# A perceiver kernel: float32r parts for the first ternary product, and fewer steps around keys, norms and value biases

## The chip, the cores and the metric

The kernel runs on one core of a Trainium2 chip. The metric is device time in microseconds of one execution of the whole program, as the median of the runs; the profile is of one further execution, taken by the hardware profiler. Engines are named as in the profile: PE (TensorE, matmuls; PEld its weight loads), DVE (VectorE), ACT (ScalarE), POOL (GpSimd), SP (SyncE, which only issues DMAs here).

## What is computed

A latent array x (128 batches, 32 rows, 256 columns) and a context (128 batches, 257 rows, 256 columns) go through two layers of three residual steps each:

```python
x = x + xattn0(context, LN(x))     # softmax attention of 32 rows on 257 context rows
x = x + ssm(LN(x))                 # gated selective scan over the 32 rows, 512 channels, 16 states
x = x + ffn0(LN(x))                # gelu(LN(x) @ Q(W_fc).T), layernorm, @ Q(W_proj).T; Q is ternary
x = x + xattn1(LN(x), context)     # linear attention with a focused feature map, 16 heads
x = x + attn1(LN(x))               # latent attention with a distance decay
x = x + ffn1(LN(x))                # 8-bit activations, ternary weights, gelu
```

Two pieces matter most for the change. The focused feature map of xattn1, on queries and keys alike, is

```python
x = relu(x) + 1e-6
x = x / softplus(scale)
n = norm(x)                 # along the 256 columns
x = x ** 3 / norm(x ** 3) * n
```

and its output is `q @ (k.T @ v) / (q . sum(k) + 1e-6)`, where `v = context @ Wv + bv`. In ffn0 the weight matrix W_fc is replaced by -1, 0 and 1 before the first product, so only the activations carry many significant bits. Inputs and outputs are float32.

## The kernel before

**Units of work.** Four batches of 32 latent rows make a *group* of 128 rows, one per partition; there are 32 groups. Groups are put together in blocks of 2, 4, 4, 4, 4, 4, 4, 4 and 2 (`BLOCKS`). For each block the program lists: for every group `context_group` (line 993: xattn0, and the keys and values of xattn1 reduced to a small tile `kvc`); then one `scan_block` (1155) for the block; then for every group `latent_group` (1471), which is `mlp` (1223, ffn0), `linear` (1259, the query side of xattn1), `attention` (1310) and `quantized_mlp` (1441). Weight preparation stands in front, and `late_setup` (882) after the first block's context.

**The order is planned ahead.** Nothing is issued when it is listed. A `Recorder` (267) notes every operation with the engines that may do it, a time for each from `ns_of` (42), and the regions of tiles that it reads and writes. `order` (403) then lays all operations out with a list scheduler that follows its own clock: each part of the work has a due time in the table `DUE`, an operation whose earliest start lies within `WINDOW` of the first possible one competes by due time, and an operation that may run on several engines goes to the one with the smallest start plus time x (1 + `PRICE`). The result is one fixed sequence per engine, and `trace` (566) issues it; the line of every such instruction is therefore 575, and the groups of the profile are told apart by tile names. `keep_busy` (553, issuing at line 562) puts dummy matmuls into gaps of PE that the planner sees as longer than 600 ns.

**Buffers.** Tiles come from rings: `t1` of 7 buffers of 1 KB a partition, `t2` of 17 of 2 KB, `t4` of 4 of 4 KB, eight PSUM banks, and small ones. How early a piece of work can begin depends also on a free buffer of its ring.

**The steps that the change touches.**
- Keys (`keys`, 1102, and `keys_values`, 1121): the product of context and key weights for one batch fills a bank (`pkey`, 128x512). The bias goes in first, as a matmul of three bf16 rows `bk3` with ones. Then `relu` on ACT into `ku`, POOL adds `e1` (1e-6 over the softplus), and `cubed` (765) follows: two squares on ACT with a sum each, the cube on POOL, two squares again, then one POOL power over the four sums `kn` (exponents 0.5 and -0.5) and one POOL product to `kf`. ACT scales the values by it into `vf`, and PE adds keys times values into `pk`.
- `kvc` is formed from `pk` on DVE; the value bias is applied later, in `linear`: DVE copies the denominators to `den`, POOL multiplies `bv1` by them, and DVE adds the numerators and multiplies by the reciprocal `zf`.
- Norms: `stats` (961) takes mean and variance on DVE, `rstd_of` (955) makes the reciprocal root in two POOL steps, and `norm` (969) applies both on DVE into `xn`. This happens for every group in the scan, in attention and in the quantized MLP.
- First ternary product (`mlp`, 1223): the centred rows are transposed by PE, copied by ACT to `xT`, and split into three bf16 parts `x3` (two casts on ACT or POOL, two subtractions on POOL). PE multiplies each part by the ternary weights, kept in bf16.

The matmuls of that product read, for each half of the 1024 columns,

```python
(x3[:, k3, dc * P : (dc + 1) * P], w_fc[:, dc, cols])
for dc in range(2) for k3 in range(3)
```

- `quantize` (1409): `qm` is 127 over the largest magnitude (a reciprocal and a multiply on DVE); for 256 columns DVE scales and rounds and POOL takes the rounding constant away again.

Of the kernel before, what the change touches and what calls it, by code (L numbers as in the profile page):

```python
# [9 lines left out]
BF16 = mybir.dt.bfloat16  # L10
I32 = mybir.dt.int32
# [255 lines left out]
class Recorder:  # L267
# [62 lines left out]
    def record(self, calls):  # L330
        ways = {}
        for engine, (name, args, kw) in calls.items():
            out = kw.get("out", args[0] if args else None)
            rest = list(args[1:] if "out" not in kw else args)
            rest += [v for k, v in kw.items() if k not in ("out", "accum_out")]
            ins = [a for a in rest if is_ap(a)]
            outs = [a for a in (out, kw.get("accum_out")) if is_ap(a)]
            full = dict(kw)
            if name == "tensor_scalar":
                full |= dict(zip(("scalar1", "scalar2"), args[2:4]))  # L340
            if name == "scalar_tensor_tensor":
                full |= dict(zip(("scalar",), args[2:3]))
            if name == "activation":
                full |= dict(zip(("func",), args[2:3]))
            if engine == "gpsimd" and name == "tensor_tensor":
                full |= dict(zip(("op",), args[3:4]))
            n = size_of(out)
            ns = ns_of(engine, name, full, out, ins, n)
            table = TABLES.get(full.get("func")) if name == "activation" else None
            tensors = [  # L350
                a for a in ins if (size_of(a) > 1 or name == "tensor_tensor") and not in_psum(a)
            ]
            locks = engine == "gpsimd" and len(ins) > 0
            if engine == "vector":
                two = name in ("tensor_tensor", "scalar_tensor_tensor", "tensor_tensor_scan")
                fast = name in ("tensor_scalar", "tensor_copy") and not in_psum(out)
                locks = len(tensors) > 1 if two else fast and len(tensors) > 0 and n > 64
            ways[engine] = [(name, args, kw)], ns, locks
        reads = [b for b in map(box_of, ins) if b]
        writes = [b for b in map(box_of, outs) if b]  # L360
        bufs = [a.buf for a in (*ins, *outs) if isinstance(a, View)]
        self.keep += bufs
        self.bufs_of.update((id(b), b) for b in bufs)
        if self.joined is not None:
            small = ins[0].shape[0] < P or size_of(ins[0]) < P
            self.joined.append((*ways["tensor"][:2], reads, writes, small))
            return
        landing = 0
        if "sync" in ways:
            size = size_of(out) * P * 4 if writes else 0  # L370
            landing = 2000 + size / 180.0
        self.add(ways, reads, writes, table, landing)
# [218 lines left out]
PRICE = {"tensor": 0.0, "vector": 28.013093, "scalar": 4.356996, "gpsimd": 3.720234, "sync": 0.0}  # L591
WINDOW = 13.821085
SOONER = 0.0675
AHEAD = 0.744939
HORIZON = 1.665209
# [3 lines left out]
def perceiver_kernel(ctx: ExitStack, tc: tile.TileContext, t: dict, out: bass.AP):  # L599
# [30 lines left out]
    nc.gpsimd.memset(halves[:, 1, :], 0.5)  # L630
    ones = cst.tile([P, P], F32, name="ones")
# [61 lines left out]
    def t2k(shape, name, dtype=F32):  # L693
        return ring("t2", 17).tile(shape, name, dtype)
# [33 lines left out]
    bv1 = row("bv1", t["bv1"], D)  # L728
# [17 lines left out]
    w_fc = wts.tile([P, 2, HID], BF16, name="w_fc")  # L746
# [18 lines left out]
    def cubed(u, n, tag, inverse=False):  # L765
# [8 lines left out]
        powers = halves[:, 0:2, 0:n] if inverse else halves[:, 1:3, 0:n]  # L774
        R.gpsimd.tensor_tensor(nrm, nrm, powers, ALU.pow)
        f = tiny(f"{tag}f", [P, n])
        R.gpsimd.tensor_tensor(f, nrm[:, 0, :], nrm[:, 1, :], ALU.mult)
# [59 lines left out]
    R.vector.tensor_tensor(bk, bk, col, ALU.mult)  # L837

    parts = t1k([P, 2, 4, 32], "bkp")
    R.gpsimd.memset(parts, 0.0)  # L840
    for k in range(3):
        part = ring("bkb", 1).tile([P, 2], "bkb", BF16)
        R.vector.tensor_copy(part, bk)
        R.vector.tensor_copy(parts[:, :, :, k], part.unsqueeze(2).to_broadcast([P, 2, 4]))
        if k < 2:
            R.vector.tensor_tensor(bk, bk, parts[:, :, 0, k], ALU.subtract)
# [24 lines left out]
    R.vector.tensor_scalar(p_l[:, 0, :], pkl[:, 0:D], 0.0, None, ALU.max)  # L871
    R.vector.tensor_tensor(p_l[:, 0, :], p_l[:, 0, :], e1, ALU.add)
# [88 lines left out]
    def stats(xg):  # L961

        st = tiny("st", [P, 6])
        R.vector.bn_stats(st, xg)
        mv = tiny("mv", [P, 2])
        R.vector.bn_aggr(mv, st)
        return mv, rstd_of(mv[:, 1:2], LN_EPS)

    def norm(xg):
        mv, r = stats(xg)  # L970
        xn = t1k([P, D], "xn")
        R.vector.tensor_scalar(xn, xg, mv[:, 0:1], r, ALU.subtract, ALU.mult)
        return xn, mv, r
# [19 lines left out]
    def context_group(b0, xg, kvc):  # L993
# [91 lines left out]
        with R.together():  # L1085
            for m in range(8):
# [6 lines left out]
                )  # L1093
        for b in range(0, GB, PAIR):
            zs = keys(cTs[b : b + PAIR])
            for i in range(PAIR):
                keys_values(cTs[b + i], zs[i], pk[:, :, b + i, :], b + i == GB - 1)
        v = pk.rearrange("p c b (h k) -> p h c b k", h=2)
        R.vector.tensor_scalar(kvc, v[:, 0], odd[:, 0:1], None, ALU.mult)
        R.vector.scalar_tensor_tensor(kvc, v[:, 1], odd[:, 1:2], kvc, ALU.mult, ALU.add)  # L1100

# [19 lines left out]
    def keys_values(cT, z, pk, last):  # L1121
        u = t2k([P, 2, D], "ku")
        R.relu(u, z)
        R.gpsimd.tensor_tensor(u, u, e1.unsqueeze(1).to_broadcast([P, 2, D]), ALU.add)
        f = cubed(u, 2, "k")
        R.first = (len(R.ops) - 3,)
# [10 lines left out]
        for j in range(2):  # L1137
            R.scalar.activation(
                vf[:, j, :, 0:16], pv[:, j * D : (j + 1) * D].rearrange("p (h k) -> p h k", k=16),
                AF.Copy, scale=f[:, j : j + 1],  # L1140
            )
        R.gpsimd.tensor_copy(vf[:, :, :, 16], f.unsqueeze(2).to_broadcast([P, 2, NH]))
        with R.together():
            for c in range(2):
                for j in range(2):
                    for m in range(4 * c, 4 * c + 4):
# [5 lines left out]
                        )  # L1152


    def scan_block(x, late):
# [3 lines left out]
        xT = ring("xTs", 1).tile([P, 2, TOK], "xTs")[:, :, 0:tok]  # L1159
        for g in range(size):  # L1160
            xn, _, _ = norm(x[g])
            R.gpsimd.tensor_tensor(x[g], x[g], b_out, ALU.add)
            transposed(xn, xT[:, :, g * P : (g + 1) * P], 2)
# [59 lines left out]
    def mlp(xg):  # L1223
# [3 lines left out]
        xT = t1k([P, D], "xT")  # L1227
        transposed(xc, xT.rearrange("p (c n) -> p c n", c=2), 2)

        x3 = t2k([P, 3, D], "x3", BF16)  # L1230
        R.cast(x3[:, 0, :], xT)
        R.gpsimd.tensor_tensor(xT, xT, x3[:, 0, :], ALU.subtract)
        R.cast(x3[:, 1, :], xT)
        R.gpsimd.tensor_tensor(x3[:, 2, :], xT, x3[:, 1, :], ALU.subtract)
# [3 lines left out]
        for k in range(2):  # L1238
            ph = bank("ph")
            cols = slice(k * 512, (k + 1) * 512)  # L1240
            with R.together():
                accumulate(ph, [
                    (x3[:, k3, dc * P : (dc + 1) * P], w_fc[:, dc, cols])
                    for dc in range(2) for k3 in range(3)
                ])
# [13 lines left out]
    def linear(xg, kvc):  # L1259
# [32 lines left out]
        den = tiny("den", [P, NH], 2)  # L1292
# [361 lines left out]
```

## Time and profile before

| | |
|---|---|
| three runs | 1712.74, 1715.9, 1718.06 us (median 1715.9) |
| span of the profiled execution | 1714.2 us |
| busy: PE, DVE, ACT, POOL | 1650.3, 1501.8, 1422.8, 1362.6 us |
| mean granted clock of PE | 0.996 of full |
| bytes moved by DMA | 59.74 MB, 35 GB/s in the mean |
| ph (first ternary product) on PE | 384 matmuls of 128x512, 91.5 us |
| POOL powers `kn`, `rstd`, `rms`, `ln` | 134.3, 126.1, 45.5, 23.3 us |

The profiled execution's own time is not listed apart from its span, which is 1.7 us below the median. Busy time counts an engine as occupied from start to end of each instruction; matmuls overlap, so the mean length of one is not the time that it costs PE. What one costs is read where many of them stand end to end. The chain of waits follows the run back from its last instruction. The "40 slices" of the page give each engine's busy share in tenths, slice by slice.

### The profile page before, as it was taken

What the parts mean: (1) busy time and instruction counts of PE and PEld (TensorE: products, weight loads), DVE (VectorE), ACT (ScalarE), POOL (GpSimd) and SP (SyncE); (2) the same over time, 40 slices, a digit from 0 to 9 for tenths busy, and PEclk for the clock granted to TensorE, in tenths of its full rate; (3) what the DMA queues carried; (4) which work ended last, traced back from release to release, by engine and by line L of the source; (5) the groups of instructions that cost most, each with busy time, mean ns of one, the idle gap of its engine ahead of it and who ended that gap; (6) DMA issues with size and microseconds to landing.
All of it is one profiled execution on the core that took longest, in us unless ns stands there. A gap on an engine that the chain in (4) does not pass through costs nothing.

```text
span 1714.2 us, 45797 instructions
## 1 busy us (share of the span) xinstructions
PE 1650.3 (96%) x17587; PEld 1200.9 (70%) x17587; DVE 1501.8 (88%) x2960; ACT 1422.8 (83%) x3484; POOL 1362.6 (79%) x2152
## 2 busy tenths in 40 slices
PE   8999999999999999999999999999999989899986
PEld 6778777767677767766777777777777666666664
DVE  5389699988997997959998997979999899999777
ACT  4587789888988899779888998889998888788676
POOL 6668769768795888688878678886898699788887
PEclk9999999999999999999999999999999999999999
DMA  8312100110010102001100012010110000000000
GB/s 235 99 60 72 30 29 30 57 35 7 29 54 5 35 14 63 30 2 45 38 30 29 8 42 63 3 29 10 61 42 30 2 20 8 4 4 2 5 9 22
DMA packets 44762, 59.74 MB, mean 35 GB/s; under 512 B 8704, under 2 KB 27008, under 8 KB 44544
## 3 DMA queue, kind: packets, MB, share of 16 engines
q1 hardware_dynamic: 44544, 56.81, 10.7%
q8 instruction: 139, 2.28, 0.6%
q14 instruction: 79, 0.65, 0.1%
HBM read 52.32 MB, written 4.19 MB: 33 GB/s over the span
## 4 chain that ended last, share of the span: by engine, by line
PE 48%; DVE 24%; ACT 15%; POOL 10%; issue 3%; DMA 0%; DVEq 0%; POOLq 0%; ACTq 0%; SPq 0%
DVE h L575 10%; PE pkey L575 7%; PE pproj L575 7%; PE pval L575 6%; DVE acc L575 5%; PE pT L575 3%; PE pmlp L575 3%; PE pqa L575 3%; POOL ku L575 3%; ACT a L575 2%; PE pk L575 2%; ACT ks L575 2%; ACT L575 2%; PE pka L575 2%; PE pcT L575 2%
## 5 line engine op out<-in xcount | busy, mean ns | idle before, releaser
L575 DVE TENSOR_TENSOR_SCAN h<-a,pproj 128x512 f32<-128x512 f32 (+1 forms) x576 | 613.9, 1087 | 22.6 <-ACT a L575 12.5
L575 ACT ACTIVATE a<-dl,a_neg 128x496 f32<-128x496 f32 (+1 forms) x576 | 367.5, 664 | 57.7 <-DVE h L575 53.6
L575 DVE SCALAR_TENSOR_TENSOR acc<-h,w_st,acc 128x512 f32<-128x512 f32 (+1 forms) x436 | 299.9, 688 | 0.7
L575 PE MATMUL pval<-wkv,cT 128*128 128x256 f32 x1024 | 243.9, 384 | 0.1
L575 PE MATMUL pkey<-wkv,cT 128*128 128x256 f32 x1024 | 238.1, 386 | 0.0
L575 ACT ACTIVATE ks<-ku 128x256 f32<-128x256 f32 x512 | 209.1, 415 | 19.3 <-POOL ku L575 17.9
L575 PEld LDWEIGHTS pkey<-wkv,cT 128*128 128x128 f32 x1024 | 189.3, 190 | 39.0 <-issue 15.6
L575 PEld LDWEIGHTS pval<-wkv,cT 128*128 128x128 f32 x1024 | 188.0, 190 | 32.0 <-issue 4.5
L575 POOL TENSOR_TENSOR ku<-ku,e 128x512 f32<-128x512 f32 x128 | 162.8, 1280 | 31.3 <-ACT ku L575 30.0
L575 POOL TENSOR_TENSOR ku<-ks,ku 128x512 f32<-128x512 f32 x128 | 164.4, 1290 | 16.9 <-ACT ks L575 15.8
L575 POOL TENSOR_TENSOR kn<-kn,halves 128x4 f32<-128x4 f32 x128 | 134.3, 1052 | 23.5 <-ACT ks L575 21.9
L575 ACT ACTIVATE vf<-pval,kf 128x256 f32<-128x256 f32 x256 | 108.3, 475 | 31.1 <-PE pval L575 26.3
L575 POOL TENSOR_TENSOR rstd<-rstd,halves 128x1 f32<-128x1 f32 x224 | 126.1, 567 | 6.1
L575 PE MATMUL pproj<-xTs,w_in 128*128 128x512 f32 (+1 forms) x288 | 122.8, 554 | 2.2 <-DVE x L575 1.3
L575 ACT ACT_TABLE_LOAD x95 | 121.9, 1283 | 2.3 <-DVE hq L575 0.6
L575 POOL TENSOR_TENSOR some<-some,h 128x512 f32<-128x512 f32 (+1 forms) x104 | 115.2, 1107 | 3.5
L575 PE MATMUL pmlp<-w_pr,hT 128*128 128x256 f32 x512 | 117.3, 383 | 0.6 <-DVE x L575 0.6
L575 PEld LDWEIGHTS pmlp<-w_pr,hT 128*128 128x128 f32 x512 | 96.2, 191 | 14.7 <-DVE x L575 0.7
L575 POOL TENSOR_SCALAR h<-h,w_st 128x512 f32<-128x512 f32 (+1 forms) x104 | 65.3, 629 | 51.0 <-DVE h L575 32.7
L575 ACT ACTIVATION_READ_ACCUMULATOR ks<-ku 128x1 f32 x512 | 100.8, 197 | 0.0
L575 POOL TENSOR_SCALAR rstd<-mv 128x1 f32<-128x1 f32 x224 | 45.4, 203 | 67.5 <-DVE mv L575 43.3
L575 PE MATMUL ph<-w_fc,x 128*128 128x512 bf16 x384 | 91.5, 380 | 0.3 <-ACT vf L575 0.2
(289 smaller groups left out, 3867.0 us busy)
## 6 DMA issues: line engine op xcount, KB each, us to landing
cx<-in_ctx_dram SPq DMA_DIRECT2D x64, 512.0 KB
x<-in_x_dram SPq DMA_DIRECT2D x32, 128.0 KB
cr<-in_ctx_dram SPq DMA_DIRECT2D x128, 32.0 KB
out_dram<-x SPq DMA_DIRECT2D x32, 128.0 KB
vlz<-vl SPq DMA_DIRECT2D x128, 1.1 KB
w_in<-in_w_inT_dram SPq DMA_DIRECT2D x1, 1024.0 KB
raw_fc<-in_w_fcT_dram SPq DMA_DIRECT2D x2, 512.0 KB
raw_pr<-in_w_prT_dram SPq DMA_DIRECT2D x2, 512.0 KB
```

What stands on the lines that cost most here:

```text
L575: ins = getattr(engine, name)(*(traced(a) for a in args), **{k: traced(v) for k, v in kw.items()}).ins
```

## The change

- First ternary product: the weights `w_fc` become float32r instead of bf16 (the tile doubles from 4 to 8 KB a partition, and the ring `t2` goes from 17 buffers to 15). The transposed rows are taken from PSUM as two float32r parts: a copy, and on DVE the difference between PSUM and that copy. PE runs 8 matmuls a group instead of 12.
- Keys: `bk3` now holds two versions of the bias, with and without `e1`. The first batch of each pair uses the one with `e1`, and one DVE maximum of the bank with `e1` takes the place of the relu and the POOL addition; the second batch stays as it was.
- `cubed`: a DVE reciprocal of one sum, a product with the other on DVE or POOL, and one POOL power 0.5, instead of a power of all sums and a product.
- Norms: the scan takes all groups' variances through one pair of POOL steps; the application of mean and root may run on DVE or POOL.
- Value bias: laid out per head in `bvc` by 16 small DMAs, and added to `kvc` (two operations on DVE or POOL); the three steps in `linear` become one DVE product.
- `quantize`: the multiply to `qm` and, for 256 columns, both steps may run on DVE or POOL.
- The planner's constants and the whole table `DUE` are different, and an operation may now stand for a list of instructions on one engine (used for `vf`, which DVE may also do, as one instruction).

```diff
-PRICE = {"tensor": 0.0, "vector": 28.013093, "scalar": 4.356996, "gpsimd": 3.720234, "sync": 0.0}
-WINDOW = 13.821085
-SOONER = 0.0675
-AHEAD = 0.744939
-HORIZON = 1.665209
+PRICE = {"tensor": 0.0, "vector": 97.062355, "scalar": 0.224837, "gpsimd": 1.848322, "sync": 0.0}
+WINDOW = 14.097169
+SOONER = 0.067381
+AHEAD = 0.41459
+HORIZON = 1.567155
...
-        return ring("t2", 17).tile(shape, name, dtype)
+        return ring("t2", 15).tile(shape, name, dtype)
...
-    bv1 = row("bv1", t["bv1"], D)
+    bvc = wts.tile([P, 2, 16], F32, name="bvc")
+    for c in range(2):
+        for h in range(8):
+            h_ = slice((c * 8 + h) * 16, (c * 8 + h + 1) * 16)
+            R.sync.dma_start(bvc[h * 16 : (h + 1) * 16, c, :], t["bv1"][:, h_].to_broadcast([16, 16]))
...
-    w_fc = wts.tile([P, 2, HID], BF16, name="w_fc")
+    w_fc = wts.tile([P, 2, HID], F32R, name="w_fc")
...
-        powers = halves[:, 0:2, 0:n] if inverse else halves[:, 1:3, 0:n]
-        R.gpsimd.tensor_tensor(nrm, nrm, powers, ALU.pow)
         f = tiny(f"{tag}f", [P, n])
-        R.gpsimd.tensor_tensor(f, nrm[:, 0, :], nrm[:, 1, :], ALU.mult)
+        R.vector.reciprocal(f, nrm[:, 1 - inverse, :])
+        R.either.tensor_tensor(f, f, nrm[:, inverse, :], ALU.mult)
+        R.gpsimd.tensor_tensor(f, f, halves[:, 1, 0:n], ALU.pow)
...
+    bks = tiny("bks", [P, 2, 2], 1)
+    R.vector.scalar_tensor_tensor(bks[:, :, 0], col, FOCUS_EPS, bk, ALU.mult, ALU.add)
+    R.vector.tensor_copy(bks[:, :, 1], bk)
...
+    def normed(xg, mv, r):
+        xn = t1k([P, D], "xn")
+        R.either.tensor_scalar(xn, xg, mv[:, 0:1], r, ALU.subtract, ALU.mult)
+        return xn
...
+        vb = t1k([P, 2, GB, 16], "vb")
+        R.either.tensor_tensor(
+            vb, bvc.unsqueeze(2).to_broadcast([P, 2, GB, 16]),
+            kvc[:, :, :, 16:17].to_broadcast([P, 2, GB, 16]), ALU.mult,
+        )
+        R.either.tensor_tensor(kvc[:, :, :, 0:16], kvc[:, :, :, 0:16], vb, ALU.add)
...
-        R.relu(u, z)
-        R.gpsimd.tensor_tensor(u, u, e1.unsqueeze(1).to_broadcast([P, 2, D]), ALU.add)
+        e12 = e1.unsqueeze(1).to_broadcast([P, 2, D])
+        if shifted:
+            R.vector.tensor_tensor(u, z, e12, ALU.max)
+        else:
+            R.relu(u, z)
+            R.gpsimd.tensor_tensor(u, u, e12, ALU.add)
...
+        mvs = tiny("mvs", [P, NG, 2], 1)
+        rs = tiny("rs4", [P, NG], 1)[:, 0:size]
         for g in range(size):
-            xn, _, _ = norm(x[g])
+            moments(x[g], mvs[:, g])
+        R.gpsimd.tensor_scalar(rs, mvs[:, 0:size, 1], LN_EPS, 1.0, ALU.add, ALU.mult)
+        R.gpsimd.tensor_tensor(rs, rs, halves4[:, 0:size], ALU.pow)
+        for g in range(size):
+            xn = normed(x[g], mvs[:, g], rs[:, g : g + 1])
...
-        x3 = t2k([P, 3, D], "x3", BF16)
-        R.cast(x3[:, 0, :], xT)
-        R.gpsimd.tensor_tensor(xT, xT, x3[:, 0, :], ALU.subtract)
-        R.cast(x3[:, 1, :], xT)
-        R.gpsimd.tensor_tensor(x3[:, 2, :], xT, x3[:, 1, :], ALU.subtract)
+        xs = [t1k([P, D], f"xT{k}", F32R) for k in range(2)]
...
+        R.copy(xs[0], pt[:, 0:D])
+        R.vector.tensor_tensor(xs[1], pt[:, 0:D], xs[0], ALU.subtract)
...
-                    (x3[:, k3, dc * P : (dc + 1) * P], w_fc[:, dc, cols])
-                    for dc in range(2) for k3 in range(3)
+                    (part[:, dc * P : (dc + 1) * P], w_fc[:, dc, cols])
+                    for dc in range(2) for part in xs
...
-        R.gpsimd.tensor_tensor(
-            yv, bv1.rearrange("p (h k) -> p h k", k=16),
-            den.unsqueeze(2).to_broadcast([P, NH, 16]), ALU.mult,
+        R.vector.tensor_tensor(
+            yv, pv[:, :, 0:16], zf.unsqueeze(2).to_broadcast([P, NH, 16]), ALU.mult
         )
-        R.vector.tensor_tensor(yv, pv[:, :, 0:16], yv, ALU.add)
-        R.vector.tensor_tensor(yv, yv, zf.unsqueeze(2).to_broadcast([P, NH, 16]), ALU.mult)
...
-        R.vector.tensor_scalar(m, m, 127.0, None, ALU.mult)
+        R.either.tensor_scalar(m, m, 127.0, 1.0, ALU.mult, ALU.mult)
...
-        engine = wide if n == HID else R.vector
+        engine = wide if n == HID else R.either
         engine.tensor_scalar(h, h, m, ROUND, ALU.mult, ALU.add)
...
-        engine = wide if n == HID else R.gpsimd
+        engine = wide if n == HID else R.either
```

## The prediction

> **What bounds the kernel now.** I read the page first: its busy shares and its 40 slices.
>
> ```profile
> span 1714.2 us, 45797 instructions
> PE 1650.3 (96%) x17587; PEld 1200.9 (70%) x17587; DVE 1501.8 (88%) x2960; ACT 1422.8 (83%) x3484; POOL 1362.6 (79%) x2152
> PE   8999999999999999999999999999999989899986
> ...
> DVE  5389699988997997959998997979999899999777
> ```
>
> The span is 1.7 us under the 1715.9 us median of the three runs (1712.74 to 1718.06); sums below are made on the span and carried to the median. TensorE (PE) leads, but a share alone can hide padding: the planner puts dummy matmuls (line 562) into gaps. So the second view was busy time by stretches, once for all instructions and once for line 562 alone:
>
> ```profile
> core 0: us, PE busy (x) PEld busy (x) DVE busy (x) ACT busy (x) POOL busy (x), PEclk, DMA share, GB/s
> 100.00:1300.00 1200.00, 1186.69 (x12689) 872.00 (x12687) 1083.98 (x2031) 1042.74 (x2608) 953.13 (x1483) 1.00 0.11 33
> 1300.00:1714.00 414.00, 368.80 (x4051) 257.98 (x4050) 365.82 (x806) 326.71 (x711) 345.64 (x558) 0.98 0.03 11
> ```
>
> From 100 to 1300 us PE is busy 98.9% of the time, line 562 runs nothing there, and the granted clock is full. In this stretch work taken from PE should shorten the run nearly one for one. After 1300 us line 562 fills 32 us (1.56 + 9.68 + 11.34 + 1.42 + 8.02 over the five stretches I asked for), so PE really works 337 of 414 us, and DVE, POOL and chains between engines share the bound.
>
> Third, the groups of instructions with shapes kept apart, for prices (columns: busy us in all, mean ns of one, idle before):
>
> ```profile
> L575 PE MATMUL ph<-w_fc,x 128*128 128x512 bf16 x384 | 91.5, 380 | 0.3 <-ACT vf L575 0.2
> L575 POOL TENSOR_TENSOR ku<-ku,e 128x512 f32<-128x512 f32 x128 | 162.8, 1280 | 31.3 <-ACT ku L575 30.0 <-DVE xn L575 0.5
> L575 POOL TENSOR_TENSOR kn<-kn,halves 128x4 f32<-128x4 f32 x128 | 134.3, 1052 | 23.5 <-ACT ks L575 21.9
> L575 DVE TENSOR_SCALAR xn<-x,mv,rstd 128x256 f32<-128x256 f32 x96 | 48.8, 522 | 20.6 <-POOL rstd L575 18.9 <-ACT ls L575 1.5
> L575 DVE TENSOR_TENSOR p<-pq,e 128x256 f32<-128x256 f32 x32 | 13.2, 413 | 0.1
> ```
>
> Matmul means are latencies of overlapped instructions, so PE's prices come from the chain of waits, where runs of them stand end to end:
>
> ```profile
> 1613.95 2.59 PE ph L575 x12
> 1421.72 1.72 PE pproj L575 x4
> ```
>
> A bf16 matmul of 512 columns takes 215 ns there, and one instruction of a float32 matmul of 512 columns 430 ns. A float32 product is two such instructions (the counts show it), so 860 ns, four times the bf16 one.
>
> **PE.** Each of 32 groups now runs 12 bf16 matmuls for the first ternary product (two dc, three parts, two halves) and will run 8 float32r ones. No row shows float32r. Bounds: 215 ns (the bf16 row, the fastest with 512 columns) and 860 ns (a full float32 product), with 430 ns (one float32 instruction) between. I take 215: a float32 product costs four bf16 ones here, and a float32r operand is one rounded part, its remainder being made by a subtract, so one part by one part is a quarter of 860. Against 12 x 215 = 2.58 us a group, 8 x 215 is 1.72 us: 0.86 us x 32 = 27.5 us less. At 430 it is 27.5 us more, at 860 137.6 us more. Weight loads (98 ns for the bf16 parts, 190 ns for float32) lie beside matmuls of 215 ns or more, so nothing; uncovered they would add 8 x 190 ns x 32 = 48.6 us. Perfetto Trace Analysis in the Trainium skill (Engine Utilization, its footnote) halves the array's output rate for FP32_LOW_HIGH, which agrees with 430 against 215 and would speak against this change if float32r fell under it; the page does not name float32r, and by that rule the sum would be +27.5 instead of -27.5 us.
>
> By windows, 22 of the 32 groups' ph matmuls lie between 100 and 1300 us (264 of 384) and 10 later. So -18.9 us on the saturated stretch; of the later 8.6 us I count half, -4.3, because PE has slack there.
>
> **DVE.** Added: 64 maxima of keys (128x512, PSUM with e1). Slope from p<-pq,e (413 ns at 256) and ea<-psa,decay (278 at 128): 1.055 ns an element, so 683 ns, 43.7 us; the nearest 512-wide row, hq<-phq, gives 739. Reciprocals: 128 of two columns at about 0.16 (156 ns for one column, 237 for 16) and 32 of one, 25.5 us. The second part xs[1], 32 x 0.413 = 13.2. Sum +82.4. Removed: xn of the three norms 48.8, the quantizer's first step at 256 columns 13.4, qm's multiply 9.2, den 5.2, one y step 13.1, and y's other step now from PSUM (518 to 410 ns) 3.3: -93.0. Net -10.6 us. I expect the steps offered to both engines on POOL: the planner multiplies an instruction's time by one plus its price, 98 for DVE and 2.8 for POOL.
>
> **POOL.** Removed: e1's add in every second batch 81.4; the power on two columns instead of four, 128 x (1.05 - 0.71, the two-column row) = 43.4; linear's power 4.6; the casts and subtractions of x3 53.1; bv1 by den 19.9; 23 of the scan's norm additions 4.7 and its powers 9.3 (32 of 567 ns against nine of up to four columns). Sum -216.4. Added: 96 xn at 0.58 (q<-xn 0.414 plus 0.166 for two column operands, the difference of dq and rstd; the wider bound is xc's 0.614) 55.7; the quantizer at 256 columns 15.2; qm 64 x 0.203 = 13.0; the value bias on kvc, 32 products and 32 sums of 128 elements, between 0.21 (kf) and 0.76 (x<-x,y), taken at 0.48, 31. Net -101.5 us. **ACT**: half the key relus (36.5) and the x casts (15.5) go, -52 us.
>
> None of these three bounds the middle stretch, so they count nothing there: PE hides them. Were the cover gone, DVE is the one near it, 1084 us in a stretch of then 1181, 92%. In the end part about ten groups each take some 1.8 us from DVE's 366 us; I allow -2 us for that and for mlp's shorter chain (two casts and two subtractions, about 2.1 us, become one DVE step of 0.41). GPSIMD Engine Reference in the Trainium skill (4.1 Engine selection) sends two-input elementwise work to VectorE and holds GpSimd about twice as slow. The rows say 278 ns on DVE against my 480 for kvc's products; by the rule they belong on DVE, 13 us cheaper on the engine but on the fuller one.
>
> Moves and queues. On SP the one load of bv1 (0.42 us of issue) becomes 16 small ones: 15 x 0.35 to 0.47 us, 5 to 7 us of issue near 22 us, ahead of wqa, woa, wupk, wupv and the second group's x and cx. The weights are used from 250 us on; the group's transposes are not, and PE ran dummies then, so 0 to 7 us; I take 0, since lighter key chains (ku and kn stand on the chain before 120 us) give 1 to 2 us back there. The reciprocal puts DVE into the chain square to f: it can stand behind a scan (1.2 us), with POOL's multiply and power, ACT's vf and PE's pk waiting, while POOL's power is 0.34 shorter: -0.2 to +1.2 us of latency a batch, hidden as long as other batches' matmuls are ready. Equally xs[1] holds a PSUM bank for DVE's turn; ph waits for it. Rings: t2 loses two of 17 buffers (x3 used one), and t1's seven also carry xT0, xT1 and vb; nothing below zero there, at worst the 64-batch price in the third rival.
>
> **Sum.** -18.9 - 4.3 - 2 = -25.2 us: span 1689.0, median about 1691.
>
> **Rivals.**
> 1. More than that: the other engines' relief also closes gaps after 1300 us. PE idles or pads there 77 us; if DVE's 18 us there come off too, and all 27.5: 1715.9 - 27.5 - 18 = 1670. For: 88% DVE with PE at 81% real work. Against: the final chain from 1640 us hops between engines, and its norms and quantizers get POOL steps.
> 2. Swallowed: PE is freed but waits as long, DVE at 92% and fewer t2 buffers keeping its matmuls late: 1713. For: three engines at 79 to 88%. Against: PE waited for others only about 13 us in 1200.
> 3. Slower by waits: each of the 64 DVE maxima, standing behind scans, delays PE by 0.9 us, 58 us less the 25: 1749; at 0.5 us 1723. It decides from 25.2 / 64 = 0.39 us a batch. Against: eight PSUM banks and other work between.
> 4. Slower, the change failing at what it says: float32r at 430 ns. +18.9 + 4.3 = 23 us, so 1739 (at 860, 84% of 137.6, 1831). Break-even where 8r = 2.58 us, r = 322 ns. For: float32 rows show 430. Against: those multiply two halves in each instruction.
>
> **How the numbers follow.** A run tells 0.3%, 5.1 us, from no change. Chances: forecast 0.66 (1680 to 1703), rival 1 0.14, rival 2 0.06, rival 3 0.07 (half of it below 1735), rival 4 0.07. Faster 0.80, same 0.06, slower 0.14. For eight in ten the range goes from 1666, under rival 1's value, to 1718, over rival 2's and the unknown queue costs; outside stay rivals 3 and 4 and a little of rival 1.
>
> **What will show it.** Right: ph 256 instructions, about 61 us busy and 215 ns apart in the chain; PE still about 98% from 100 us to some 1280; POOL near 1261, DVE near 1491, ACT near 1371. The forecast is wrong if ph's instructions stand over 322 ns apart, if PE's idle time in the middle stretch grows from 13 to over 30 us (look for pk, pval or ph waiting for DVE's reciprocal, ku or xT1), or if the stretch after the last context group grows beyond 300 us.

## The result, and the profile after

The changed kernel takes 1762.35 us (median of four runs, 1758.68 to 1763.55) against 1716.98 us for the kernel before on the same chip: a ratio of 1.0265, interval 1.025 to 1.0281. It is 45 us slower; the forecast was 1691 us, 25 us faster, with a range that ended at 1718.

The profiled execution took 1758.68 us. From its page, the head, two of the 40-slice rows, and the chain by engine and by line:

```profile
span 1756.7 us, 45618 instructions
...
PE 1641.9 (93%) x17416; PEld 1209.0 (69%) x17444; DVE 1497.9 (85%) x2962; ACT 1384.6 (79%) x3381; POOL 1318.8 (75%) x2178
...
PE   8999999999999989999999999999999998998885
...
POOL 4665738757687759687678786877779867989997
...
PE 39%; POOL 24%; DVE 20%; ACT 9%; issue 5%; DMA 1%; SPq 0%; POOLq 0%; DVEq 0%; ACTq 0%
PE pkey L586 8%; DVE h L586 8%; PE pval L586 6%; POOL xn L586 5%; DVE acc L586 5%; PE pproj L586 5%; POOL rstd L586 3%; PE pT L586 2%; POOL ku L586 2%; POOL some L586 2%; ACT a L586 2%; POOL x L586 2%; PE pk L586 2%; PE pmlp L586 2%; PE pqa L586 2%
```

Every engine is busy for less time than before, PE by 8.4 us and POOL by 43.8, and yet the run is longer: the time went into waiting. POOL, the engine with the lowest busy share, holds 24% of the chain of waits, and a line that was not there before, `POOL xn`, holds 5%. Before, POOL held 10%:

```profile
PE 48%; DVE 24%; ACT 15%; POOL 10%; issue 3%; DMA 0%; DVEq 0%; POOLq 0%; ACTq 0%; SPq 0%
```

The slices hide it: PE's row still reads nine nearly throughout, and POOL's goes up and down between 3 and 9. (The helper's line is now 586, the dummies' 573; in the experiments below it is 587 or 576.)

Busy time by stretches, the two that the prediction used:

```profile
core 0: us, PE busy (x) PEld busy (x) DVE busy (x) ACT busy (x) POOL busy (x), PEclk, DMA share, GB/s
100.00:1300.00 1200.00, 1155.64 (x12207) 857.68 (x12217) 1061.69 (x1998) 986.82 (x2449) 873.86 (x1427) 1.00 0.10 33
1300.00:1714.00 414.00, 369.16 (x4251) 267.69 (x4256) 348.39 (x747) 320.16 (x725) 355.14 (x573) 0.98 0.04 12
```

Between 100 and 1300 us PE is idle for 44 us, where it was idle for 13; and 5.4 us of its busy time there are now dummy matmuls, where there were none. No other engine took its place as the busiest: all of them fell. The groups that the change touched (busy in all, mean ns of one, idle before):

```profile
L586 POOL TENSOR_TENSOR kf<-kf,halves 128x2 f32<-128x2 f32 x128 | 92.3, 723 | 4.0
L586 POOL TENSOR_SCALAR xn<-x,mv,rstd 128x256 f32<-128x256 f32 x64 | 78.3, 1223 | 2.5
L586 PE MATMUL ph<-w_fc,xT 128*128 128x512 f32 x256 | 75.9, 423 | 1.4 <-DVE xT L586 0.7 <-ACT qT L586 0.5
L586 DVE TENSOR_TENSOR ku<-pkey,e 128x512 f32<-128x512 f32 x64 | 43.2, 675 | 6.8 <-PE pkey L586 4.9 <-POOL some L586 1.9
L586 POOL TENSOR_SCALAR xn<-x,mvs,rs 128x256 f32<-128x256 f32 x32 | 40.0, 1254 | 0.3
```

All 96 steps `xn` went to POOL, and each takes 1.23 us there; on DVE it took 0.522. The planner's own formula (`ns_of`) gives POOL 0.557 us for it, so the order was laid out for a step less than half as long as it is. Who waits for it:

```profile
PEld pT L586 <- POOL xn L586: 33.0, 37, 2.4
...
PE pT L586 <- POOL xn L586: 21.3, 31, 1.6
...
DVE amax L586 <- POOL xn L586: 20.1, 19, 2.5
```

The chain of waits shows what such a stretch looks like (start, us, what). The last line, a little later, is the first ternary product:

```profile
736.45 0.56 POOL rstd L586
737.01 0.67 POOL rms L586
737.68 1.21 POOL xn L586
...
742.53 1.04 POOL rs L586
743.57 0.68 POOL rms L586
744.25 1.22 POOL xn L586
...
749.51 1.29 POOL xn L586 x2
...
754.34 1.20 POOL xn L586
...
771.97 1.22 POOL xn L586
773.24 0.87 PE pT L586 x6
...
780.62 2.05 PE ph L586 x8
```

From 736 to 776 us six of these `xn` stand among POOL's root, norm and quantizer steps, and the next matmuls wait for the end of that queue. Busy times in that stretch, which is 40 us out of 1757:

```profile
736.00:776.00 40.00, 34.53 (x367) 24.62 (x366) 21.31 (x55) 24.52 (x51) 37.48 (x67) 1.00 0.03 8
```

POOL is busy 94% of it, DVE 53%. An engine that is 75% busy over the run is the bound here. Two waits of PE's weight loads grew most between 100 and 1300 us: `pT` for POOL's `xn` takes 19.6 us, and `pk` for POOL's `vf` 17.7 us, where it took 6.6 before. The last values-times-keys matmul `pk` ends at 1477.4 us before and 1512.3 us after (same view of both):

```profile
L575 PE MATMUL pk<-vf,ku x4096: 192/196/220, 62.5 to 1477.4; 128*32 128x34 f32 x196
```

```profile
L586 PE MATMUL pk<-vf,ku x4096: 191/196/220, 52.3 to 1512.3; 128*32 128x34 f32 x196
```

So 34.9 of the 42.5 us of longer span are lost before the last context group is through, and 7.6 after it (236.8 us from there to the end before, 244.4 after). The loss sits in the middle stretch, where the forecast had its gain.

### The profile page after: what moved, and what is told of

Its sections match the earlier page's. It is cut to its first block, busy times and chain, and to the rows that moved or that the text cites. A ratio compares the mean times of both kernels' runs of the same rounds, so it can differ in the third digit from the quotient of the medians.

```text
span 1756.7 us, 45618 instructions
## 1 busy us (share of the span) xinstructions
PE 1641.9 (93%) x17416; PEld 1209.0 (69%) x17444; DVE 1497.9 (85%) x2962; ACT 1384.6 (79%) x3381; POOL 1318.8 (75%) x2178
## 4 chain that ended last, share of the span: by engine, by line
PE 39%; POOL 24%; DVE 20%; ACT 9%; issue 5%; DMA 1%; SPq 0%; POOLq 0%; DVEq 0%; ACTq 0%
PE pkey L586 8%; DVE h L586 8%; PE pval L586 6%; POOL xn L586 5%; DVE acc L586 5%; PE pproj L586 5%; POOL rstd L586 3%; PE pT L586 2%; POOL ku L586 2%; POOL some L586 2%; ACT a L586 2%; POOL x L586 2%; PE pk L586 2%; PE pmlp L586 2%; PE pqa L586 2%
## 5 line engine op out<-in xcount | busy, mean ns | idle before, releaser
L586 POOL TENSOR_TENSOR ku<-ku,e 128x512 f32<-128x512 f32 x64 | 82.3, 1286 | 67.8 <-ACT ku L586 67.6
L586 POOL TENSOR_TENSOR rstd<-rstd,halves 128x1 f32<-128x1 f32 x192 | 107.3, 561 | 5.8
L586 POOL TENSOR_TENSOR kf<-kf,halves 128x2 f32<-128x2 f32 x128 | 92.3, 723 | 4.0
L586 POOL TENSOR_SCALAR rstd<-mv 128x1 f32<-128x1 f32 x192 | 37.9, 197 | 72.8 <-DVE mv L586 42.8
L586 DVE BATCH_NORM_STATS2 st<-x 128x6 f32<-128x256 f32 x192 | 78.3, 413 | 7.3 <-POOL x L586 5.7
```

What stands on the lines that cost most here:

```text
L586: ins = getattr(engine, name)(*(traced(a) for a in args), **{k: traced(v) for k, v in kw.items()}).ins
```

## The experiments

The runs were set against these ideas. First: POOL's `xn` is the cause. Second: the waits put into the key chain (the DVE maxima of the third rival, and the reciprocals) are. Beside them: float32r's price, and what work taken from one engine is worth at all.

Laying the work out anew changes everything at once, so nearly every experiment keeps the planned order: the planner sees the kernel as it was, and only when an operation is issued are other instructions put in its place. The device is one edit in `trace`, the same in all runs but one, and not shown again below:

```diff
...
-            for name, args, kw in op.ways[op.engine][0]:
+            planned = [(op.engine, *c) for c in op.ways[op.engine][0]]
+            for on, name, args, kw in getattr(op, "instead", planned):
+                engine = getattr(self.nc, on)
...
```

### Is it xn on POOL?

**e1**: the changed kernel, `xn` issued on DVE.

```diff
+        R.ops[-1].instead = [("vector", "tensor_scalar",
+            (xn, xg, mv[:, 0:1], r, ALU.subtract, ALU.mult), {})]
```

> The changed kernel with its fixed order of instructions kept as it is; only the 96 instructions that apply mean and root (xn) run on DVE, at their place in the order, instead of POOL. Theory 1 (xn on POOL is the loss: 1.22 us there where the plan's formula, 195 + 2 x 75 + 0.83 x 256, allows 0.56, and PE, DVE and ACT wait for it): 1762 falls to 1690 to 1715, PE's idle time between 100 and 1300 us falls from 44 to under 25 us. Theory 2 (the new DVE steps in the key chain, maximum and reciprocal, are the loss): it stays above 1745, since DVE gets 96 x 0.4 to 0.5 = 38 to 48 us more work. Theory 3 (float32r at 256 ns and two buffers fewer): stays at 1750 to 1765.

1726.23 us, 1.0056 of before (1.0035 to 1.0077), 36 us less than as changed, although DVE now carries 37 us more than in the changed kernel. It falls short of what the first idea was given (1715 at most), and PE is still idle for 32 us between 100 and 1300 us, not for under 25. The same 40 us of the run as above, in which the work is not quite the same:

```profile
736.00:776.00 40.00, 38.70 (x429) 27.25 (x429) 31.27 (x75) 30.24 (x61) 32.81 (x59) 1.00 0.03 8
```

PE's share goes from 86% to 97%, POOL's from 94% to 82%.

**e2**: the opposite edit, the kernel before with its 96 `xn` on POOL and nothing else changed.

```diff
+        R.ops[-1].instead = [("gpsimd", "tensor_scalar",
+            (xn, xg, mv[:, 0:1], r, ALU.subtract, ALU.mult), {})]
```

> The kernel before with its own fixed order; only xn's 96 instructions run on POOL instead of DVE. Theory 1: slower by 30 to 60 us, 1745 to 1775, from POOL's 96 x 1.22 = 117 us against DVE's 49. Theories 2 and 3: no change beyond 10 us, since neither of their causes is in it.

1761.98 us, 1.0269 (1.0254 to 1.0284). This one edit makes the kernel before as slow as the whole change does. Its `xn` group, its busy times, and the chain by engine:

```profile
L576 POOL TENSOR_SCALAR xn<-x,mv,rstd 128x256 f32<-128x256 f32 x96 | 120.8, 1260 | 1.5 <-PE pka L576 0.2
```

```profile
100.00:1300.00 1200.00, 1164.03 (x12228) 850.95 (x12270) 1040.50 (x1921) 1024.03 (x2547) 999.14 (x1504) 1.00 0.10 32
```

```profile
POOL 33%; DVE 25%; PE 22%; ACT 13%; issue 5%; DMA 2%; SPq 1%; POOLq 0%; DVEq 0%; ACTq 0%
```

PE's idle time grows from 13 to 36 us with its work untouched, and POOL leads the chain with 33%, while its busy share in the stretch is 83%.

**e3**: the changed kernel, `xn` on POOL as x times the root, without the mean.

```diff
+        R.ops[-1].instead = [("gpsimd", "tensor_scalar", (xn, xg, r, 0.0, ALU.mult, ALU.add), {})]
```

> The changed kernel, fixed order kept, xn left on POOL but with one column operand (x times the root); the subtraction of the mean is left out, so only the instruction's price changes, near 0.47 us as the quantizer's one-column step at 256 columns measured. Theory 1, in its form that the price of this one instruction is the loss: 1690 to 1715, about the same as with xn on DVE. If it is the engine rather than the price: over 1740. Theories 2 and 3: 1750 to 1765.

1710.61 us, 0.9963 (0.9951 to 0.9976): with a short `xn` in the same place, the changed kernel is a little faster than the kernel before.

```profile
L587 POOL TENSOR_SCALAR xn<-x,rstd 128x256 f32<-128x256 f32 x64 | 30.5, 477 | 2.3
...
L587 POOL TENSOR_SCALAR xn<-x,rs 128x256 f32<-128x256 f32 x32 | 15.5, 494 | 0.3
```

```profile
100.00:1300.00 1200.00, 1179.81 (x12659) 882.07 (x12677) 1087.61 (x2058) 1012.28 (x2521) 852.91 (x1470) 1.00 0.11 34
```

PE's idle time is back to 20 us. The first idea is right in this form: the length of the step is what counts, not that POOL does it.

**e8, e11, e18**: three ways to keep the whole computation. e8: POOL forms a column nb = -mean x root, then x times root plus nb. e11: DVE turns the mean's sign, POOL adds it and multiplies. e18: DVE forms nb, ACT applies both.

```diff
+            ("gpsimd", "tensor_scalar", (nb, mv[:, 0:1], r, -1.0, ALU.mult, ALU.mult), {}),
+            ("gpsimd", "tensor_scalar", (xn, xg, r, nb, ALU.mult, ALU.add), {}),
...
+            ("vector", "tensor_scalar", (nm, mv[:, 0:1], -1.0, None, ALU.mult), {}),
+            ("gpsimd", "tensor_scalar", (xn, xg, nm, r, ALU.add, ALU.mult), {}),
...
+            ("vector", "tensor_scalar", (nb, mv[:, 0:1], r, -1.0, ALU.mult, ALU.mult), {}),
+            ("scalar", "activation", (xn, xg, AF.Identity), {"bias": nb, "scale": r}),
```

> The changed kernel, fixed order kept, xn on POOL with two column operands in the other form, x times root plus a column of minus mean times root, made by one more small POOL instruction of about 0.3 us. If two columns as such make the slow instruction: still about 1.22 us each, 1762 to 1790. If the subtract as first operation makes it: 0.5 to 0.65 us each, 1712 to 1730.

> The changed kernel, fixed order kept, xn on POOL as an addition and a product with two columns: DVE first turns the sign of the mean's column (about 0.15 us), off the chain that POOL's root is on. If only the subtract makes the slow instruction: about 0.55 us each, 1710 to 1725. If any addition or subtraction as first operation with two columns does: 1.2 us each, 1755 to 1770.

> The changed kernel in its fixed order, with its whole computation: xn by ACT as x times root plus a column that one DVE step forms (mean x root x -1), instead of POOL's 1.23 us step. POOL loses 118 us, ACT gains about 96 x 0.42 = 40 (price of the 256-column activation ls) and DVE 96 x 0.16 = 15. If the POOL step's length is what made the change slower, the time falls to that of the run with one column on POOL plus the added DVE step in the chain (96 x 0.16 at most, about half of it on the path): 1710 to 1722, no slower than the kernel before. If any move out of the planned place costs as much (ACT's queue holds xn behind scans' exponentials), it stays above 1735.

```profile
L587 POOL TENSOR_SCALAR xn<-x,rstd,nb 128x256 f32<-128x256 f32 x64 | 35.2, 550 | 6.9
...
L587 POOL TENSOR_SCALAR nb<-mv,rstd 128x1 f32<-128x1 f32 x64 | 17.1, 267 | 4.9
```

```profile
L587 POOL TENSOR_SCALAR xn<-x,nm,rstd 128x256 f32<-128x256 f32 x64 | 35.5, 555 | 23.6 <-DVE nm L587 14.8 <-DVE ea L587 1.5 <-PE pkey L587 1.4
```

```profile
L587 ACT ACTIVATE xn<-x,nb,rstd 128x256 f32<-128x256 f32 x64 | 38.0, 597 | 24.7 <-DVE nb L587 19.9 <-DVE qm L587 2.6 <-DVE zf L587 1.9
```

Two operands by column are not what makes the step slow: multiply-add and add-multiply with two columns take 0.55 to 0.57 us. Only subtract-then-multiply takes 1.22 to 1.26. All six forms in the changed kernel's order:

| form of `xn` | us of one | us of the kernel | ratio to before |
|---|---|---|---|
| POOL, subtract and multiply (as changed) | 1.23 | 1762.35 | 1.0265 |
| e18: DVE column 0.20, ACT 0.60 | 0.80 | 1741.03 | 1.0147 |
| e8: POOL column 0.27, POOL 0.55 | 0.83 | 1737.49 | 1.0133 |
| e11: DVE sign 0.14, POOL 0.56 | 0.70 | 1729.53 | 1.0063 |
| e1: DVE | 0.53 | 1726.23 | 1.0056 |
| e3: POOL, one column, no mean | 0.48 | 1710.61 | 0.9963 |

The second column adds the steps' times; in e11 the sign can be turned while POOL makes the root, and the row shows that `xn` still had to wait for it (14.8 us in all for these 64). e1, e8 and e11 came out 11, 7 and 5 us above the ranges expected of them, and e18 missed by more (1710 to 1722): it takes 113 us off POOL, yet ACT's `xn` waits 26.8 us for DVE's column and POOL waits 47.3 us for ACT's `xn`. The table says that time in this chain costs the kernel a good part of itself, wherever it is spent. None of the five that keep the whole computation is as fast as the kernel before.

**e4**: `xn` written for DVE alone, and the planner lays the work out anew with the changed kernel's due times.

```diff
-        R.either.tensor_scalar(xn, xg, mv[:, 0:1], r, ALU.subtract, ALU.mult)
+        R.vector.tensor_scalar(xn, xg, mv[:, 0:1], r, ALU.subtract, ALU.mult)
```

> The changed kernel with xn written for DVE alone, so that the planner lays everything out anew with the same due times and constants. Theory 1 alone would give about 1700. If the due times fit only the set of instructions that they were made for, it is far slower, 1780 to 1850, and then runs with a new layout can't be used to price a single part.

1861.99 us in its one run, 136 us more than the same instructions in the old order (e1). A new layout swings the time by more than any part of the change, so such a run prices the layout and not the part.

### Is it the key chain?

Both runs start from e1 and put one old piece back. e6: the power of all four sums and the product after it, no reciprocal. e7: relu and POOL's addition of `e1` for every batch, with the bias rows to match.

```diff
         R.vector.reciprocal(f, nrm[:, 1 - inverse, :])
+        R.ops[-1].instead = []
         R.either.tensor_tensor(f, f, nrm[:, inverse, :], ALU.mult)
+        R.ops[-1].instead = [("gpsimd", "tensor_tensor", (nrm, nrm, powers, ALU.pow), {})]
         R.gpsimd.tensor_tensor(f, f, halves[:, 1, 0:n], ALU.pow)
+        R.ops[-1].instead = [("gpsimd", "tensor_tensor", (f, nrm[:, 0, :], nrm[:, 1, :], ALU.mult), {})]
...
             R.vector.tensor_tensor(u, z, e12, ALU.max)
+            R.ops[-1].instead = [("scalar", "activation", (u, z, AF.Relu), {}),
+                                 ("gpsimd", "tensor_tensor", (u, u, e12, ALU.add), {})]
...
-                r = slice(i * 32, i * 32 + 3)
+                r = slice(32, 35)
```

> The changed kernel, fixed order kept, xn on DVE (1726), and the factor of cubed as before: one POOL power over all sums and a POOL product, no DVE reciprocal between them. Theory 2 (the reciprocal's wait in DVE's queue delays the key chain): 1705 to 1720. If the reciprocal is covered and POOL's longer power counts: 1726 to 1740.

> The changed kernel, fixed order kept, xn on DVE (1726), and the keys of every batch as before: relu on ACT and e1's addition on POOL, 64 more of each, instead of 64 maxima on DVE. Theory 2 (the maxima stand behind scans in DVE's queue): 1700 to 1720. If the lighter keys are worth what POOL and ACT save: 1735 to 1770.

e6: 1738.15 us, 12 more than e1. e7: 1801.73 us, 75 more than e1. Both pieces of the change are worth having in this order, and the second idea falls. With the old keys, of which POOL and ACT have twice as many, POOL's waits for ACT's `ku` grow from 72.4 us in e1, and those of ACT's squares for POOL from 15.4:

```profile
POOL ku L587 <- ACT ku L587: 101.0, 54, 13.1
ACT ks L587 <- POOL ku L587: 69.6, 97, 1.9
```

The 75 us are no price for the kernel before, whose order was laid out with the long keys in it; they say what this order counts on.

### Is it float32r?

**e5** is e1 and **e12** is e3, each with two bf16 parts in place of the two float32r ones (what the third part held is left out).

```diff
-    w_fc = wts.tile([P, 2, HID], F32R, name="w_fc")
+    w_fc = wts.tile([P, 2, HID], BF16, name="w_fc")
...
-        xs = [t1k([P, D], f"xT{k}", F32R) for k in range(2)]
+        xs = [t1k([P, D], f"xT{k}", BF16) for k in range(2)]
```

> The changed kernel, fixed order kept, xn on DVE (1726 us so far), and the two parts and the ternary weights in bf16 instead of float32r, eight matmuls as before, so the third part of the rows is left out. Only the matmul's type differs. If the shortfall of float32r (256 ns an instruction in the chain of waits, 215 forecast) costs the run: 256 x 41 ns = 10.5 us, 1714 to 1719. If it is hidden in waits: 1722 to 1729.

> The changed kernel, fixed order kept, xn on POOL with one column (the mean's subtraction left out, 1711 us so far) and the two parts of the first ternary product in bf16 (the third part left out). With xn at the plan's price PE idles less than with xn on DVE, so float32r's 41 ns more an instruction may count now: 1699 to 1705 if all 10.5 us do, 1708 to 1712 if they are hidden again.

e5: 1724.99 us against 1726.23 of e1; e12: ratio 0.9961 (0.9946 to 0.9977) against 0.9963 of e3. Eight float32r matmuls take 2.05 us (the chain's line above), 256 ns each and not the 215 of bf16, 10.5 us over the run; none of it shows in the time (the intervals are some 3 us to either side). The kernel before with float32r alone was not run.

### What is work taken from one engine worth?

Five runs on the kernel before, in its order. e9: 8 instead of 12 bf16 matmuls (third part left out). e13: the largest hidden magnitude taken over 128 of 1024 columns on DVE. e14: POOL's addition of `s0` left out. e15: ACT's sum of squares over 128 columns. e16: these four together.

```diff
...
+                for dc in range(2) for k3 in range(2)
...
+            ("vector", "tensor_reduce", (amax2, hid[:, 0:128], AX.X, ALU.max), ...
...
         R.gpsimd.tensor_tensor(xg, xg, s0, ALU.add)
+        R.ops[-1].instead = []
...
+            ("scalar", "activation", (junk[:, 0:128], hid[:, 0:128], AF.Square), ...
```

> The kernel before with its fixed order; the first ternary product runs 8 bf16 matmuls a group instead of 12 (the third part of the rows is made but left out of the product), nothing else differs. It takes exactly the 27.5 us from PE that the prediction took. If PE bounds the stretch to 1300 us as the prediction had it: 1716 falls by 15 to 25 us, to 1691 to 1701. If PE's 98.9% is held up by the others as much as by its own work: 1708 to 1716.

> The kernel before, fixed order; the quantizer's maximum over the 1024 hidden columns reads 128 of them, which takes some 32 x 1.0 = 32 us from DVE and nothing else (the other 896 columns are left out of the maximum). If DVE is what bounds the middle stretch, where PE's 27.5 us were worth about 4: 1717 falls by 20 to 32 us. If no single engine bounds it: by 0 to 10 us.

> The kernel before, fixed order; POOL's addition of s0 to x in every group is left out, 24.3 us less on POOL. If POOL bounds: 15 to 24 us faster. If no single engine bounds it: 0 to 8 us.

> The kernel before, fixed order; the square and sum over the 1024 hidden columns reads 128 of them, some 32 x 0.83 = 27 us less on ACT (the other 896 columns are left out of the sum). If ACT bounds: 15 to 27 us faster. If no single engine bounds it: 0 to 8 us.

> The three edits together and the eight matmuls a group instead of twelve: 27.5 us less on PE, 32 on DVE, 24 on POOL, 27 on ACT. If the engines hold each other, each with waits that another fills, the four together give clearly more than the sum of the four alone: 20 to 30 us. If one engine alone bounds, they give about what that one gave.

| | taken away | ratio to before | us |
|---|---|---|---|
| e9 | PE 27.5 us | 0.9981 (0.997 to 0.9991) | -3.3 |
| e13 | DVE 30 us | 0.9991 (0.9979 to 1.0003) | -1.5 |
| e14 | POOL 24 us | 0.9995 (0.9983 to 1.0006) | -0.9 |
| e15 | ACT 24 us | 0.9994 (0.9985 to 1.0004) | -1.0 |
| e16 | all, 106 us | 0.9935 (0.9913 to 0.9957) | -11.2 |

What e13, e14 and e15 take away is read from the shortened or missing rows (less than the 32 and 27 expected of e13 and e15). The last column is the ratio's distance from 1 times the median of before; the intervals of e13 to e15 include no change at all, and e16 stays under the 20 to 30 us that were expected of engines holding each other. e9 is the main term of the forecast, measured by itself in the order from which its price and its stretch were read:

```profile
100.00:1300.00 1200.00, 1172.49 (x12591) 865.10 (x12591) 1082.82 (x2030) 1041.36 (x2604) 951.00 (x1484) 1.00 0.10 33
```

PE's busy time in the stretch falls by 14.2 us, and its idle time rises from 13.3 to 27.5: PE waits instead. The others' work came no earlier.

**e17**: the opposite, 16 matmuls instead of 12.

```diff
...
+                for dc in range(2) for i, k3 in enumerate((0, 1, 2, 2))
```

> The kernel before in its fixed order, with 16 bf16 matmuls a group for the first ternary product instead of 12 (the third part is multiplied twice, so the product counts it double): 27.5 us more on PE by the forecast's 215 ns. If PE's work sets the time one for one, as the forecast took it, some 23 us are added (22 groups x 0.86 in the saturated stretch, half of the rest): 1740. If the order has room for PE in both directions (taking four away was worth 3.3 us), 3 to 8 us are added: 1721 to 1725. If lateness costs fully where earliness gains little, 20 us or more are added although four fewer gained 3.3.

1732.32 us, 1.0093 (1.0076 to 1.0109): 16 us more for 27.5 us of work, where 27.5 less gave 3.3; it lies between the two outcomes foreseen, 8 and 20.

```profile
100.00:1300.00 1200.00, 1188.46 (x12574) 873.83 (x12616) 1077.15 (x2010) 1035.42 (x2587) 943.29 (x1469) 1.00 0.11 33
```

```profile
PE 59%; DVE 18%; ACT 12%; POOL 8%; issue 3%; ACTq 0%; DVEq 0%; POOLq 0%
```

Now PE has 59% of the chain (48% before). PE and POOL were each made later (e17, e2) and were waited for; each of the four made earlier by itself brought 3.3 us or less, and in e9 PE's idle time took the place of its work. That fits a kernel that stands at a balance of its engines. e16 is above the sum of its parts (6.7 us), but within the noise of both; even 106 us of engine time bring 11.

## Why the prediction was wrong

**The sum's PE term, -18.9 and -4.3.** This step failed: "In this stretch work taken from PE should shorten the run nearly one for one." The price of float32r was a smaller miss (256 ns for 215, so 12 x 215 - 8 x 256 = 0.53 us a group for 0.86). The rule was the larger one: at the full 27.5 us less, e9 gained 3.3. That was measured in the order of before; in the new order the relief was not run by itself. A busy share of 98.9% was read as if PE alone were the bound. The page's chain of waits gave PE 48%, not all, and asked for the same stretch it begins with a line of DVE:

```profile
by line: DVE h L575 11.5%; PE pkey L575 8.0%; PE pproj L575 7.6%; PE pval L575 7.4%; DVE acc L575 5.6%; POOL ku L575 3.2%; PE pT L575 3.1%; issue 3.0%; PE pk L575 2.4%; PE pqa L575 2.4%; ACT ks L575 2.4%; ACT a L575 2.3%; PE pmlp L575 2.1%;
```

For this stretch the forecast used the chain for prices only. The other direction was dearer: 16 us for 27.5 us more (e17).

**The POOL line, 96 `xn` at 0.58.** This term was mis-sized: the runs show 1.23 us. The sum of the columns was right in itself (0.55 to 0.57 for multiply-add and add-multiply, e8 and e11): which operations are done made the difference, and no row of before had subtract-then-multiply on POOL. The wider bound, `xc`'s 0.614, is a row of another instruction (TENSOR_TENSOR, with the column repeated), and the slowest POOL row of 256 columns, `x<-x,y`, takes 0.762: no row of this size would have bounded the step. A price without a row of its form needed a rival of its own. Priced like `ku<-ku,e`, 1.28 us at 512 columns, 96 steps take 67 us more than at 0.58; waited for, they would have taken the range past 1750.

GPSIMD Engine Reference in the Trainium skill (4.1 Engine selection), which the prediction drew on for kvc's products, calls one-input work on GpSimd roughly line-rate. The multiply-add form agrees (0.55 us against 0.522 for DVE's `xn`); the subtract form takes 2.4 times DVE's time and does not.

**"None of these three bounds the middle stretch, so they count nothing there: PE hides them."** This failed for POOL, and it is where the sign was lost. POOL's busy time did fall, by 43.8 us instead of 101.5 (the difference of 57.7 is the 62.6 of `xn`, less small gains elsewhere). But `xn` stands at the head of each of the chains through scan, attention and quantized MLP, between a wait for the root and PE's transposes, and in stretches like 736 to 776 us POOL is the bound whatever its share of the run. An average does not hide a step that is waited for.

**The account.** 1691 was forecast and 1762 measured, 71 us apart. The price of `xn` accounts for 33 us (against e11, near the 0.58 of the forecast but with a wait for DVE added) to 52 (against e3, which is a little shorter and lacks the mean). The PE term, worth 3 instead of 23, accounts for some 20. The rest, 0 to 18 us, stays open: the new order as a whole, the two `t2` buffers fewer and the later start are in it, and no run separates them (e4). With a step near the forecast's price (e3, e1, e11) the kernel took between 1711 and 1730, not 1691: about even with the kernel before, or a little slower.

**Rivals.** Slower came true, and by a wait, but not the third rival's: the 64 maxima take 675 ns (683 forecast), DVE idles 6.8 us before them, and the lighter keys help (e7). The fourth didn't happen: 256 ns is under its break-even of 322, and the parts' kind is not seen in the time (e5, e12). "Swallowed" was right on the mechanism of the PE term (e9) and had been given 6%. What was missing is a rival for a step moved to an engine that is waited for in its chain, with the step's price as the open quantity.

**What would show it.** The sign named in advance did show: PE's idle time in the middle stretch grew over 30 us (44). Its cause was looked for at `pk`, `pval` and `ph` behind DVE; the largest part is at the transposes `pT` behind POOL's `xn`, and `pk` comes next, behind POOL's `vf` and not behind DVE. PE's 98% to some 1280 us did not come (96.3% of the middle stretch), and `ph` took 75.9 us at 256 ns instead of 61 at 215. Right in size were the reciprocal (150 ns), the power on two columns (723 for 710), kvc's steps (444 for 480), `xT`'s subtraction (409 for 413) and, with small misses, DVE (1497.9 for 1491) and ACT (1384.6 for 1371). The 16 loads of `bvc` take 7.38 us of SP, for 5 to 7 forecast. They start at 26.84 us, so they are not why the first `pkey` starts at 26.4 us instead of 22.4; what either costs was not run by itself.

## What to carry to other kernels

A busy share near 100% does not say what less work on that engine gains: in a planned order with several engines near the limit, read the chain of waits of the stretch, and expect little from a relief of one engine (here 3.3 us of 27.5). Before a step is moved to another engine, look for a row of exactly its form there (instruction, operations, operands). If none exists, rows of its size are no bound (here the slowest took 0.76 us and the step 1.23): run the step first, or carry its price as a rival; a planner's price for it deserves the same doubt. Then ask who waits for the step, because an engine that is 75% busy over the run can be the bound in the stretch where it counts.

## What was unexpected in the hardware

- A POOL step on 256 columns with two operands by column takes 1.22 to 1.26 us as subtract-then-multiply and 0.55 to 0.57 us as add-then-multiply or multiply-then-add; on DVE subtract-then-multiply takes 0.46 to 0.57. Why is not known from these runs. `xc`, in which POOL subtracts a repeated column by another instruction (TENSOR_TENSOR), takes 0.61 us.
- A float32r matmul of 512 columns takes 256 ns where a bf16 one takes 215, and its weight load 189 ns, as float32's, against 98 for bf16.
- The mean granted clock of PE was 0.996 of full before and 0.987 after. TensorE: Matmul & The Clock Gate in the Trainium skill (Part 1) names two states by PE's own activity, full and half rate, set in windows of some 3.4 us. The traces agree: in stretches of 10 us the lowest value after is 0.50, and 0.83, which is 3.4 us at half rate, comes up seven times in before, after and e3. By that the means stand for 14 and 46 us at half rate (1 minus the mean, times the span, times two). But this is not where the 45 us went: between 100 and 1300 us it is only 7 us after (none before), the same 7 us stand in e3, which is 52 us faster with a mean of 0.986, and some 29 us lie after 1660 us.
